# Moving statistics and GpSimd sums behind TensorE's inputs in a four-layer graph kernel, memsets to VectorE, and the last batch taken tile by tile

## The chip, the cores and the metric

The kernel runs on one core of a Trainium2 chip. The metric is the device time of one execution in microseconds. A core has TensorE (PE in the profile; its weight loads are PEld), VectorE (DVE), ScalarE (ACT), GpSimd (POOL) and SyncE (SP), which here issues all the transfers. Each engine works through its own queue in order and waits at an instruction until that instruction's inputs are there.

## What is computed

The input x has 32 batches of 512 tokens with 128 features; adj is a 512 by 512 matrix. Four layers follow each other, each of the form x = x + f(relu(layernorm(x))), with layernorm over the features:

```python
# layer 0: A = softmax of an edge table spread over adj; M = identity
out = einsum('ij,bjg->big', A * M, h @ W[0]) + einsum('ij,bjg->big', A * (1 - M), h @ W[1]) + bias
# layer 1: two Chebyshev hops with adj (both matrices are adj, so terms are shared)
out = relu(concat(h, adj_T h, (2 adj_T adj_T - 1) h, ...) @ Theta1 + bias)
# layer 2: weights = adj * adj, elementwise
features = relu(h @ psi_w + psi_b); messages = einsum('nm,bnd->bmd', weights, features)
out = relu(concat(messages, h) @ phi1_w + phi1_b) @ phi2_w + phi2_b
# layer 3: attention
A = exp(8 * tanh((h @ q) (h @ k)^T / sqrt(128) / 8)) * adj; out = (A / rowsum(A)) @ h @ v
```

## The kernel before

Two batches make a pair; there are 16 pairs (NQ = 16), q or r counting them. Tokens lie in four tiles (NT = 4) of 128 partitions. All matrix products are f32.

A layer's work on a pair is: statistics of each token (`stats_steps`: four BATCH_NORM_STATS2 on VectorE, L197, a square root on ScalarE, L209, a reciprocal and one multiply on VectorE, L211 and L212); the normalised tile h (eight activations on ScalarE, L225); a turn to feature-major hT (`turn_steps`: two VectorE transposes, L259, and a trip through DRAM); then matrix products. The statistics for the next layer are taken when a layer has updated x.

The products with the 512 by 512 matrices use Strassen's scheme with seven products in place of eight. `right_steps` (L300, GpSimd) makes four sums of blocks of the moving side; `sum_steps` (L285) makes four sums of blocks of the matrix, once for each matrix. `products` runs the seven in a fixed order, 1, 6, 5, 7, 2, 4, 3, over three PSUM banks a, c, d. Products 6, 7 and 4 share bank c, so product 7 (the fourth in order) can only start when VectorE has read product 6 out of the bank, and that reading adds what was read of product 1.

The run has two parts.

Up to L917 the order on each engine is the source's order. It prepares the attention matrix and runs layer 0 pair by pair in `round0(r)`, r = 0 to 14. In a round, `evict` reads the products: for product 1, L693 on VectorE adds the bias into u and L694 on GpSimd adds it to x; for product 6, L696 and L697; for product 7, L701, L702 and L703; products 2, 4 and 3 get a second part from `diagonal` (L684 on TensorE, with the tiles hd) and are added to x in L706, L709 and L712; a last diagonal is added in L764. hd of the next pair is made by `diagonal_of` (L636, GpSimd, two multiplications of 128 by 512). Between the products, the source puts in slices of other pairs' work with `go(steps, n)`: `ahead[q]` are the statistics for layer 0 of pair q from 4 on, `stats5` is `ahead[r + 5]`, `own[r]` the statistics of the pair just finished, `nxt` the block sums for round r + 1. From round 4 on, `sums_ahead` makes one sum of the adj or cheb matrix on GpSimd per round; layer 1 uses these.

After L917 a planner orders the instructions, with the order of the source as priority. `layer1`, `layer2` and `layer3` are generators, one for each pair; a loop at the end starts one more pair in each step and lets each active generator go on to its next `yield`. Layer 1 of pair 15 and layer 2 of pair 0 start in the same step. In `layer1` the last stage is the projection, y (L814), the update of x (L815), and `ln_stats`. In `layer2` the names are feat (projection p_feat on TensorE, L828 on VectorE, relu L829 on ScalarE), rt_feat (the block sums on GpSimd), msgT (the seven products, evicted by ScalarE L337 and L345 and VectorE L339, L341, L347, L349, L356), and h1T (L845 on ScalarE, from p_phi, L843 and L844). In `layer3` each batch has qkh and hv in one tile (copies L863 and L868 on VectorE, a column of ones for the row sums set by a memset, L867), the scores (p_score L873, tanh L874, exp L876), the product with adj (L878, by turns on VectorE and GpSimd), and p_av (L886), divided by its row sum (L888 reciprocal, L891 multiply and add) and stored.

Of the kernel before, what the change touches and what calls it, by code (L numbers as in the profile page):

```python
# [24 lines left out]
def kernel(  # L25
# [37 lines left out]
    nc = tc.nc  # L63
    B, N, D = x.shape
    NT = N // P
    NE = e_l0.shape[1]
    NK = NE // P
    NQ = B // 2
# [8 lines left out]
    def bank(name):  # L77
        return psum.tile([P, 512], F32, tag="bank", name=name)
# [27 lines left out]
    xt = []  # L106
# [80 lines left out]
    def ln_stats(q):  # L187
        for _ in stats_steps(q):
            pass
# [190 lines left out]
    def bias(q):  # L380
        x11 = xt[q][:, 0, 0:2, :]
        nc.gpsimd.tensor_add(x11, x11, spread(b0, 2))
# [14 lines left out]
    def go(steps, n=99):  # L397
        for _ in range(n):
            if next(steps, steps) is steps:
                return  # L400
# [125 lines left out]
    p = bank("p_qk_t")  # L526
# [51 lines left out]
    p = bank("p_qk")  # L578
# [28 lines left out]
    p = bank("p_adiag")  # L607
# [43 lines left out]
    ahead = {q: stats_steps(q) for q in range(4, NQ)}  # L651
# [17 lines left out]
    def diagonal_of(q):  # L669
        src = hT[f"hT0_{q}"] if q > 2 else hT[q]  # L670
        hd[q] = [straight(src, b, adiag, f"hd_{q}_{b}") for b in range(2)]

    def round0(r):

        now = rights.pop(r)

        def x_of(I, b):
            return xt[r][:, b, 2 * I : 2 * I + 2, :]  # L680

        def diagonal(p, I, b, first):
            for i in range(2):
                nc.tensor.matmul(p[:, i * D : (i + 1) * D], hd[r][b][:, blk(2 * I + i)], w0[:, 0, :],  # L684
                                 start=(first and i == 0), stop=True, skip_group_check=True)

        u = work.tile([P, 3, 2, D], F32, tag="u", name=f"u_l0_{r}", bufs=2)
        held = {}

        def evict(k, p):  # L690
            pv = p[:, :H].rearrange("p (i f) -> p i f", i=2)
            if k == 1:
                nc.vector.tensor_add(u[:, 0], pv, spread(b0, 2))  # L693
                nc.gpsimd.tensor_add(x_of(1, 0), x_of(1, 0), u[:, 0])  # L694
            elif k == 6:
                nc.vector.tensor_add(u[:, 1], pv, u[:, 0])  # L696
                nc.gpsimd.tensor_add(x_of(0, 1), x_of(0, 1), u[:, 1])  # L697
            elif k == 5:
                held["d"] = pv
            elif k == 7:  # L700
                nc.vector.tensor_add(u[:, 2], pv, u[:, 0])  # L701
                nc.vector.tensor_add(u[:, 2], held["d"], u[:, 2])  # L702
                nc.gpsimd.tensor_add(x_of(1, 1), x_of(1, 1), u[:, 2])  # L703
            elif k == 2:
                diagonal(p, 0, 0, False)
                nc.vector.tensor_add(x_of(0, 0), pv, x_of(0, 0))  # L706
            elif k == 4:
                diagonal(p, 1, 0, False)
                nc.vector.tensor_add(x_of(1, 0), pv, x_of(1, 0))  # L709
            elif k == 3:  # L710
                diagonal(p, 0, 1, False)
                nc.vector.tensor_add(x_of(0, 1), pv, x_of(0, 1))  # L712

        stats5 = ahead.get(r + 5, iter(()))
        nxt = right_of(r + 1) if r + 1 < NQ else iter(())
        if r == 0:
            diagonal_of(0)
            go(ln[3])
            go(pieces[2])
            h[3] = normed_tile(3)  # L720
            normal3 = normed_steps(3, h[3])
            go(normal3, 4)
            go(ahead[4], 2)
        else:
            if r + 4 < NQ:
                normalise(r + 4)
            go(own[r - 1], 1)
            go(nxt, 2)
        for i, _ in enumerate(products(f"l0_{r}", by_token, sums["att"], now, evict)):
            if i == 0:  # L730
                if r == 0:
                    go(ahead[4], 2)
                else:
                    go(stats5, 1)
            elif i == 1:
                if r == 0:
                    go(stats5, 2)
                else:
                    go(nxt)
                    if r + 3 < NQ:  # L740
                        turn(r + 3)
            elif i == 2:
                go(stats5, 1)
            elif i == 3 and r == 0:
                go(stats5, 1)
            elif i == 4:
                if r == 0:
                    go(turned[2], 1)
                    go(turned[2])
                    go(normal3)  # L750
                    go(ahead[4], 1)
                    go(stats5, 1)
                else:
                    if r + 3 < NQ:
                        go(turn(r + 3))
                    go(own.pop(r - 1))
            elif i == 5:
                if r == 0:
                    turn(3)
                else:  # L760
                    go(stats5, 2)
        p = bank(f"p_l0_{r}_e")
        diagonal(p, 1, 1, True)
        nc.vector.tensor_add(x_of(1, 1), p[:, :H].rearrange("p (i f) -> p i f", i=2), x_of(1, 1))  # L764
        own[r] = stats_steps(r)
        if r == 0:
            go(turn(3))
            go(nxt)
            go(own[r], NT)
            go(ahead[4])  # L770
        go(stats5)
        if r > 0:
            go(own[r], NT)
        if r + 2 < NQ:
            go(projection(r + 2))
        if r == 0:
            normalise(4)
        if r < 2:
            go(pieces[3], 1)
        elif r == 2:  # L780
            go(pieces[3])
        if r + 1 < NQ:
            bias(r + 1)
            if r >= 4:
                go(sums_ahead, 1)
            diagonal_of(r + 1)
        if r == 3:
            nc.gpsimd.tensor_add(th12, th[:, 1:3, :], th[:, 3:5, :])
        if r + NQ // 2 < NQ:
            loads(r + NQ // 2)  # L790
# [6 lines left out]
    def layer1(q):  # L797
        h = normed(q)
        yield
        hT = transposed(h, f"hT1_{q}")  # L800
        right = right_blocks(lambda J, b: h[:, b, 2 * J : 2 * J + 2, :], f"h_{q}", [nc.gpsimd] * 4)
        yield
        x1T = pair_tile(f"x1T_{q}").rearrange("p (b w) -> p b w", b=2)
        x2T = pair_tile(f"x2T_{q}").rearrange("p (b w) -> p b w", b=2)
        mixes = (mixed(f"x1T_{q}", sums["adj"], right, x1T), mixed(f"x2T_{q}", sums["cheb"], right, x2T))
        for _ in zip(*mixes):
            pass
        hs = [straight(hT, b, None, f"hs_{q}_{b}") for b in range(2)]
        yield
        for b in range(2):  # L810
            po = projected(f"p_l1_{q}_{b}", (columns(hs[b]), th[:, 0, :]), (columns(x1T[:, b]), th12[:, 0, :]),
                           (columns(x2T[:, b]), th12[:, 1, :]))
            y = late.tile([P, NT, D], F32, tag="y", name=f"y1_{q}_{b}", bufs=2)
            nc.vector.tensor_add(y, po, spread(b1, NT))  # L814
            nc.vector.scalar_tensor_tensor(xt[q][:, b], y, 0.0, xt[q][:, b], OP.max, OP.add)  # L815
        ln_stats(q)

    def layer2(q):
# [33 lines left out]
    def layer3(q):  # L852
# [5 lines left out]
        for b in range(2):  # L858
# [5 lines left out]

            pv = projected(f"p_hv_{q}_{b}", (at(hT, b), vw))
            hv = both[:, N : N + NT * (D + 1)].rearrange("p (t f) -> p t f", f=D + 1)
            nc.gpsimd.memset(hv[:, :, D : D + 1], 1.0)  # L867
            nc.vector.tensor_copy(hv[:, :, :D], pv)  # L868
            yield
            ex = square_tile(f"ex_{q}_{b}")  # L870
# [8 lines left out]
            yield  # L879
            out_r = out[2 * q + b].rearrange("(t p) f -> p t f", p=P)  # L880
            rsum = stats.tile([P, NT], F32, tag="rsum", name=f"rsum_{q}_{b}", bufs=4)
            for i0 in range(0, NT, 2):
                po = bank(f"p_av_{q}_{b}_{i0}").rearrange("p (i f) -> p i f", i=2)
                for i in range(2):
                    for t in range(NT):
                        nc.tensor.matmul(po[:, i, : D + 1], ex[:, t, blk(i0 + i)], hv[:, t, :],  # L886
                                         start=(t == 0), stop=(t == NT - 1))
                nc.vector.reciprocal(rsum[:, i0 : i0 + 2], po[:, :, D])  # L888
                for i in range(2):
                    xi = xt[q][:, b, i0 + i, :]  # L890
                    nc.vector.scalar_tensor_tensor(xi, po[:, i, :D], rsum[:, i0 + i : i0 + i + 1], xi,  # L891
                                                   OP.mult, OP.add)
                if b == 1 and q == NQ - 1:
                    nc.sync.dma_start(out_r[:, i0 : i0 + 2, :], xt[q][:, b, i0 : i0 + 2, :])
            if not (b == 1 and q == NQ - 1):
                nc.sync.dma_start(out_r, xt[q][:, b])

    adjTx = []
# [67 lines left out]
```

## Time and profile before

| What | Value |
|---|---|
| time, median of 3 runs | 980.47 us (980.4 to 980.68) |
| span of the profiled run | 979.2 us |
| time of the profiled run | 981.21 us |
| granted TensorE clock | 1.0 |
| f32 rate of TensorE, read from the starts | 0.89 us for 8 matmuls of 128 columns, 0.86 us for 4 of 256 |
| layer 0 rounds | from 40 to 196 us |
| layers 1, 2 and 3 | from 196, 475 and 686 us |

How it is read: the page gives each engine's busy time, a matmul's end being modelled. A list of waits names, for each instruction, the time that its engine stood idle just before it and which instruction's semaphore ended that. A timeline prints start, duration, engine, line, operation, output and inputs, shapes, a count of merged instructions, and in brackets the idle time before with its releaser. Where an instruction waits for several semaphores, the last one is named, and the name can be wrong if that engine only happened to finish then.

### The profile page before, as it was taken

What the parts mean: (1) busy time and instruction counts of PE and PEld (TensorE: products, weight loads), DVE (VectorE), ACT (ScalarE), POOL (GpSimd) and SP (SyncE); (2) the same over time, 40 slices, a digit from 0 to 9 for tenths busy, and PEclk for the clock granted to TensorE, in tenths of its full rate; (3) what the DMA queues carried; (4) which work ended last, traced back from release to release, by engine and by line L of the source; (5) the groups of instructions that cost most, each with busy time, mean ns of one, the idle gap of its engine ahead of it and who ended that gap; (6) DMA issues with size and microseconds to landing.
All of it is one profiled execution on the core that took longest, in us unless ns stands there. A gap on an engine that the chain in (4) does not pass through costs nothing.

```text
span 979.2 us, 16183 instructions
## 1 busy us (share of the span) xinstructions
PE 966.5 (99%) x5925; PEld 802.1 (82%) x5926; DVE 596.7 (61%) x1386; ACT 467.2 (48%) x1057; POOL 412.4 (42%) x551
## 2 busy tenths in 40 slices
PE   8999999999999999999999999999999999999998
PEld 4799999999999999999967777777667777777776
DVE  8788888755565655557566766556655444444444
ACT  3765445222322323238676544545674455444553
POOL 4778999841316313121244433344142332223322
PEclk9999999999999999999999999999999999999999
DMA  9255553522121221334343333332222121121111
GB/s 257 92 139 158 159 135 104 151 85 67 44 76 55 65 65 44 87 87 123 93 118 119 95 103 105 87 84 68 71 71 75 44 76 55 55 76 44 55 33 44
DMA packets 83023, 87.17 MB, mean 89 GB/s; under 512 B 6784, under 2 KB 73088, under 8 KB 82944
## 3 DMA queue, kind: packets, MB, share of 16 engines
q1 hardware_dynamic: 82944, 86.14, 31.4%
q8 instruction: 47, 0.77, 0.3%
q14 instruction: 32, 0.26, 0.1%
HBM read 44.70 MB, written 41.42 MB: 88 GB/s over the span
## 4 chain that ended last, share of the span: by engine, by line
PE 93%; POOL 2%; DMA 1%; ACT 1%; issue 1%; DVE 1%; SPq 0%; DVEq 0%; POOLq 0%; ACTq 0%
PE p_av L886 12%; PE p_l L372 11%; PE p_score L873 11%; PE p_msgT_c L319 4%; PE p_x2T_c L319 4%; PE p_x1T_c L319 4%; PE p_l_c L326 4%; PE p_feat L372 3%; PE p_x1T_a L319 3%; PE p_hv L372 3%; PE p_x1T_d L319 3%; PE p_x2T_d L319 3%; PE p_x2T_a L319 3%; PE p_msgT_d L319 3%; PE p_msgT_a L319 3%; PE p_qkh L860 3%
## 5 line engine op out<-in xcount | busy, mean ns | idle before, releaser
L225 ACT ACTIVATE h<-x,sh,rs 128x128 f32<-128x128 f32 x448 | 182.5, 483 | 73.2 <-PE p_x2T_d L319 43.9
L878 POOL TENSOR_TENSOR ex<-ex,adjTx 128x512 f32<-128x512 f32 x64 | 83.3, 1303 | 197.1 <-issue 147.4
L874 ACT ACTIVATE ex<-p_score 128x512 f32<-128x512 f32 x128 | 71.6, 588 | 122.9 <-issue 113.0
L886 PEld LDWEIGHTS p_av<-qkh_hv,ex 128*128 128x128 f32 x1024 | 118.4, 191 | 9.6 <-issue 7.2
L886 PE MATMUL p_av<-qkh_hv,ex 128*128 128x129 f32 x1024 | 120.3, 275 | 0.9 <-POOL qkh_hv L867 0.6
L873 PE MATMUL p_score<-qkh_hv,hT 128*128 128x512 f32 x256 | 115.2, 593 | 0.0
L259 DVE STREAM_TRANSPOSE hb_hT<-h 128x512 f32<-128x512 f32 x122 | 84.4, 698 | 19.8 <-ACT h L225 19.6
L878 DVE TENSOR_TENSOR ex<-ex,adjTx 128x512 f32<-128x512 f32 x64 | 45.9, 717 | 76.5 <-ACT ex L876 76.5
L873 PEld LDWEIGHTS p_score<-qkh_hv,hT 128*128 128x128 f32 x256 | 46.2, 190 | 46.5 <-issue 45.0
L197 DVE BATCH_NORM_STATS2 bn<-x 128x6 f32<-128x256 f32 x224 | 83.2, 417 | 1.3
L300 POOL TENSOR_TENSOR rt_h<-h 128x256 f32<-128x256 f32 x32 | 22.6, 727 | 133.4 <-PE p_x2T_c L319 133.1
L876 ACT ACTIVATE ex<-ex 128x512 f32<-128x512 f32 x128 | 76.5, 631 | 1.8
L300 POOL TENSOR_TENSOR rt_feat<-feat,feat 128x256 f32<-128x256 f32 x16 | 11.6, 727 | 128.4 <-ACT feat L829 128.4
L372 PE MATMUL p_l<-th,x2T 128*128 128x128 f32 x256 | 49.5, 275 | 0.0
L372 PE MATMUL p_l<-th,x1T 128*128 128x128 f32 x256 | 49.5, 275 | 0.0
L372 PE MATMUL p_l<-th,hs 128*128 128x128 f32 x256 | 49.5, 275 | 0.0
L372 PEld LDWEIGHTS p_hv<-vw,hT 128*128 128x128 f32 x256 | 33.6, 192 | 15.3 <-issue 8.1
L209 ACT ACTIVATE sd<-bn,eps 128x8 f32<-128x8 f32 x60 | 17.9, 300 | 56.0 <-DVE bn L197 55.0
L634 POOL COPY hs<-hT 128x512 f32<-128x512 f32 x32 | 19.6, 611 | 54.7 <-PE p_l L372 40.5
L345 ACT COPY x1T<-p_x1T_a 128x256 f32<-128x256 f32 x16 | 6.0, 372 | 74.2 <-PE p_x1T_a L319 74.2
L636 POOL TENSOR_TENSOR hd<-hT,adiag 128x512 f32<-128x512 f32 x32 | 40.6, 1287 | 1.0 <-PE p_l_e L684 1.0
L372 PEld LDWEIGHTS p_l<-th,hs 128*128 128x128 f32 x256 | 40.0, 192 | 0.8
(241 smaller groups left out, 2188.7 us busy)
## 6 DMA issues: line engine op xcount, KB each, us to landing
d_hT<-hb_hT SPq DMA_DIRECT2D x244, 128.0 KB, 2.4
hT<-d_hT SPq DMA_DIRECT2D x61, 512.0 KB, 3.7
x<-in_x_dram SPq DMA_DIRECT2D x28, 256.0 KB, 4.3
out_dram<-x SPq DMA_DIRECT2D x28, 256.0 KB, 2.3
adj_s<-in_adj_dram SPq DMA_DIRECT2D x4, 256.0 KB, 4.9
adjT_d<-adjT SPq DMA_DIRECT2D x1, 1024.0 KB
sq<-in_adj_dram SPq DMA_DIRECT2D x4, 256.0 KB
x_last<-in_x_dram SPq DMA_DIRECT2D x4, 256.0 KB
```

What stands on the lines that cost most here:

```text
L197: nc.vector.bn_stats(st[:, k].rearrange("p e s -> p (e s)"), xt[q][:, b, t : t + 2, :].rearrange("p t f -> p f t"))
L225: nc.scalar.activation(h[:, b, t, :], xt[q][:, b, t, :], AF.Relu, bias=shift[q][:, i : i + 1], scale=scale[q][:, i : i + 1])
L259: nc.vector.transpose(hb[:, :, b].rearrange("p j t r -> p t j r"), h[:, b].rearrange("p t (j c) -> p t j c", c=QR))
L319: nc.tensor.matmul(p[:, :H], b[:, k, :], a[:, k, :], start=(first and k == 0), stop=(k == 1), skip_group_check=True)
L326: nc.tensor.matmul(p[:, i * D : (i + 1) * D], a[:, k, blk(i)], b[:, k, :], start=(first and i == 0 and k == 0), stop=(k == 1), skip_group_ ...
L372: nc.tensor.matmul(p[:, blk(t)], hT(t), w, start=(i == 0), stop=(i == len(terms) - 1))
L636: nc.gpsimd.tensor_mul(split(s), src, split(scale))
L873: nc.tensor.matmul(ps, hT[:, t, b, :], qkh, start=True, stop=True)
L874: nc.scalar.activation(ex[:, t, :], ps, AF.Tanh, scale=1.0 / (8.0 * math.sqrt(D)))
L876: nc.scalar.activation(ex[:, t, :], ex[:, t, :], AF.Exp, scale=8.0)
L878: eng.tensor_mul(ex[:, t, :], ex[:, t, :], adjTx[0][:, t, :])
L886: nc.tensor.matmul(po[:, i, : D + 1], ex[:, t, blk(i0 + i)], hv[:, t, :], start=(t == 0), stop=(t == NT - 1))
```

## The change

The statistics that stood ahead of round 0's first evictions on VectorE move behind the evictions of the second and the fourth product. From round 4 on, the sum for layer 1 moves behind the hd multiplications on GpSimd. Layer 1 of pair 15 takes its statistics two steps of the loop later, so that they are not ahead of what layer 2's second pair needs. The memset of the ones column goes from GpSimd to VectorE. The last batch is divided, added and stored one tile of 128 tokens at a time and not two. The purpose is to have what TensorE waits for done first, and a shorter end.

```diff
             go(normal3, 4)
-            go(ahead[4], 2)
         else:
...
-            if i == 0:
-                if r == 0:
-                    go(ahead[4], 2)
-                else:
-                    go(stats5, 1)
+            if i == 0 and r > 0:
+                go(stats5, 1)
             elif i == 1:
                 if r == 0:
-                    go(stats5, 2)
+                    go(ahead[4], NT)
                 else:
...
-            elif i == 2:
+            elif i == 2 and r > 0:
                 go(stats5, 1)
             elif i == 3 and r == 0:
-                go(stats5, 1)
+                go(stats5, NT)
...
             bias(r + 1)
+            diagonal_of(r + 1)
             if r >= 4:
                 go(sums_ahead, 1)
-            diagonal_of(r + 1)
...
+        if q == NQ - 1:
+            yield
+            yield
         ln_stats(q)
...
-            nc.gpsimd.memset(hv[:, :, D : D + 1], 1.0)
+            nc.vector.memset(hv[:, :, D : D + 1], 1.0)
...
-            for i0 in range(0, NT, 2):
-                po = bank(f"p_av_{q}_{b}_{i0}").rearrange("p (i f) -> p i f", i=2)
-                for i in range(2):
+            final = b == 1 and q == NQ - 1
+            n = 1 if final else 2
+            for i0 in range(0, NT, n):
+                po = bank(f"p_av_{q}_{b}_{i0}").rearrange("p (i f) -> p i f", i=2)[:, :n]
+                for i in range(n):
...
-                if b == 1 and q == NQ - 1:
-                    nc.sync.dma_start(out_r[:, i0 : i0 + 2, :], xt[q][:, b, i0 : i0 + 2, :])
-            if not (b == 1 and q == NQ - 1):
+                if final:
+                    nc.sync.dma_start(out_r[:, i0, :], xt[q][:, b, i0, :])
+            if not final:
                 nc.sync.dma_start(out_r, xt[q][:, b])
```

More of the change, by code (lines that the diff above doesn't have):

```diff
@@ L887, in layer3 @@
                                          start=(t == 0), stop=(t == NT - 1))
-                nc.vector.reciprocal(rsum[:, i0 : i0 + 2], po[:, :, D])
-                for i in range(2):
+                nc.vector.reciprocal(rsum[:, i0 : i0 + n], po[:, :, D])
+                for i in range(n):
                     xi = xt[q][:, b, i0 + i, :]
```

## The prediction

> **What bounds the kernel now.** I read the page's busy shares, then TensorE's own waits, then the timelines of all engines around each wait, and the end of the run.
>
> ```profile
> PE 966.5 (99%) x5925; PEld 802.1 (82%) x5926; DVE 596.7 (61%) x1386; ACT 467.2 (48%) x1057; POOL 412.4 (42%) x551
> ```
>
> TensorE has 966.5 of 979.2 us. Only its waits can be won, and few are left:
>
> ```profile
> PE p_adjT L405 <- DMA adj_s<-in_adj_dram: 4.6, 2, 3.4
> PE p_msgT_c L319 <- POOL rt_feat L300: 1.4, 1, 1.4
> PE p_l_c L326 <- DVE u_l L696: 1.2, 1, 1.2
> PE p_av L886 <- POOL qkh_hv L867: 0.6, 1, 0.6
> PE p_l_c L326 <- POOL hd L636: 0.5, 1, 0.5
> ```
>
> The first is the load at the start, untouched here. The others are what the change aims at: layer 2, round 0, layer 3, round 4. An engine's idle time is counted from the end of the last matmul; the loss of cadence is a little larger.
>
> Round 0, timeline of VectorE, then of TensorE:
>
> ```profile
> 41.70 0.75 DVE L197 BATCH_NORM_STATS2 bn<-x 128x6 f32<-128x256 f32 x2
> 42.37 0.40 DVE L693 TENSOR_TENSOR u_l<-p_l_a,b 128x256 f32<-128x256 f32 x1
> 42.69 0.75 DVE L197 BATCH_NORM_STATS2 bn<-x 128x6 f32<-128x256 f32 x2
> 43.37 0.40 DVE L696 TENSOR_TENSOR u_l<-p_l_c,u_l 128x256 f32<-128x256 f32 x1
> ```
>
> ```profile
> 43.91 1.13 PE L326 MATMUL p_l_c<-rt_g,attT 128*128 128x128 f32 x8 [1.24 <-DVE u_l L696]
> ```
>
> Four statistics stand before the two evictions that the fourth product needs. But the next round shows the same matmul with nothing to spare, behind a VectorE queue that does not depend on TensorE:
>
> ```profile
> 52.93 0.18 DVE L211 RECIPROCAL rs<-sd 128x8 f32<-128x8 f32 x1
> 53.15 0.92 DVE L212 SCALAR_TENSOR_TENSOR sh<-bn,rs 128x8 f32<-128x8 f32 x1
> 54.21 1.08 DVE L212 SCALAR_TENSOR_TENSOR sh<-bn,rs 128x8 f32<-128x8 f32 x1
> 55.89 0.41 DVE L696 TENSOR_TENSOR u_l<-p_l_c,u_l 128x256 f32<-128x256 f32 x1
> ```
>
> ```profile
> 52.78 2.49 POOL L636 TENSOR_TENSOR hd<-hT,adiag 128x512 f32<-128x512 f32 x2
> ```
>
> L696 ends at 56.30 and its matmul starts at 56.44, where TensorE's preceding product ended (55.51 + 0.89 = 56.40).
>
> Layer 2, second pair, on VectorE, ScalarE, GpSimd and TensorE:
>
> ```profile
> 488.85 0.42 DVE L197 BATCH_NORM_STATS2 bn<-x_last 128x6 f32<-128x256 f32 x1
> 489.78 1.08 DVE L197 BATCH_NORM_STATS2 bn<-x_last 128x6 f32<-128x256 f32 x3
> 491.11 0.67 DVE L828 TENSOR_TENSOR feat<-p_feat,psib 128x512 f32<-128x512 f32 x1
> ```
>
> ```profile
> 491.74 0.69 ACT L845 ACTIVATE h1T<-p_phi,phi1b 128x512 f32<-128x512 f32 x1 [0.54 <-PE p_phi L844]
> 492.32 1.14 ACT L829 ACTIVATE feat<-feat 128x512 f32<-128x512 f32 x2
> ```
>
> ```profile
> 493.54 0.73 POOL L300 TENSOR_TENSOR rt_feat<-feat,feat 128x256 f32<-128x256 f32 x1 [8.87 <-ACT feat L829]
> ```
>
> ```profile
> 495.69 1.13 PE L319 MATMUL p_msgT_c<-sums_sq,rt_feat 128*128 128x256 f32 x4 [1.41 <-POOL rt_feat L300]
> ```
>
> The projection p_feat ran from 488.03 to 489.8, yet its first VectorE add starts at 491.11, behind the statistics of pair 15. That lateness runs through ScalarE and GpSimd to TensorE.
>
> **What the Trainium skill says.** "Perfetto Trace Analysis", Identifying the Most-Contended Engine, holds that matmul busy share doesn't measure headroom; weight loads at 82% agree, so I work from gaps in the cadence, not from the 99%. "SBUF — State Buffer", Who interferes with whom: a VectorE instruction with two SBUF inputs contends with a GpSimd instruction that reads SBUF, and the later one blocks for the whole instruction. The trace agrees: L212, 128x8 elements, takes 150 ns at best, but here 0.92 and 1.08 us, ending at 54.07 and 55.29, where the two hd multiplications of GpSimd end (half of 2.49 us each, to 54.03 and 55.27).
>
> **The change part by part.**
>
> *Round 0.* The statistics ahead[4] and stats5 go behind the evictions of the second and fourth product. VectorE is then free at 41.77 when the last sum L285 (1.22 us from 40.55) ends: L693 from 41.70 to 42.10, L696 to 42.43, and 0.14 us later, as now (43.77 to 43.91), the matmul: 42.57. That removes 43.91 - 42.57 = 1.34 us. The eight statistics then fill VectorE to about 46, before L706, for which nobody waits; TensorE keeps the lead (0.1 us less at p_g, since ScalarE's copies of hT sit behind normalisations that wait for GpSimd's sh at 46.78) and reaches round 1's fourth product near 55.2. There L696 still ends at 56.30. Its queue: the second transpose L259 at 50.99 waits for ScalarE's h, which waited for sh, which GpSimd makes after hd(0); GpSimd has no idle time over 0.1 us from 34 to 57; then 1.38 us of own statistics, and L212 twice blocked by hd(1). None of it is moved. I cost this edit at 0: the wait returns one round later, 1.2 us long.
>
> *Rounds 4 and later.* hd goes before the sum L285. hd for round 5 ends at 98.22; its first reader, L684, starts at 100.11, so hd has no one waiting. The sums are read in layer 1 only. VectorE's L212 is blocked at a round's end by whichever GpSimd operation is running, and the two are alike (a sum 1.27 to 1.30, an hd 1.26 to 1.27), so the boundaries stay. Total of the small waits in rounds 5 to 15: under 1 us. The wait of round 4 itself (TensorE at 88.33) lies before the first sum (94.46), and L696, which ended at 88.18, explains it better than the named hd. Taken: 0, from -0.7 to +0.3.
>
> *Layer 2.* The statistics of pair 15 go two steps later, four at some 0.34 us apart. Four products wait: TensorE wanted p_msgT_c at 493.25 + 0.86 = 494.11 and got it at 495.69 (1.58); restarted at 0.96 in place of 0.86 (0.10); its next p_msgT_c, wanted at 497.51, came at 497.75 (0.24) and again restarted slowly (0.10). Sum 2.02. After: L815 of the second batch at 488.97 (now 489.19), L349 at 489.6, the two adds L828 at 489.9 and 490.5, done 491.15. ScalarE then has feat ready at 490.6 and 491.2, before h1T at 491.74, and should take both first: done 491.8. GpSimd starts at 491.9; its third operation, the one that TensorE needs (2.09 us after the start, 493.54 to 495.63), ends at 494.0, just before 494.11. I take 1.9 of 2.02. The moved statistics have a home: VectorE is idle from 494.92 to 497.27, and pair 15's next reader comes many steps later.
>
> *Memsets to VectorE.* 32 of 104 ns leave GpSimd. In layer 3 the wait at 702.27 is laid to one, but it ran at 702.15, just behind the multiplication that ended at 702.22 and that TensorE needs; the memset for this tile ran at 681.8. On VectorE no row shows it: between 65 ns, an estimate from the page "VectorE: DVE Perf Modes", The TRN2 errata (58 cycles plus the elements, at 0.96 GHz), and 172 ns, the longest reciprocal of 128x2 (L888). I take 0.1; 3.2 us in all, hidden in VectorE's idle time of layer 3 (busy 4 to 5 tenths, 76.5 us of waits before L878 alone). The buffer's wait is on long finished matmuls. On the path: 0.
>
> *Last batch by tiles.* Now the last reciprocal starts at 975.52 and two multiply-adds end at 976.34; with one tile it is one, ending at 976.08 (0.26 less). The last transfer is 64 KB for 128 KB: its packets now occupy the DMA engines from 977.2 to 977.85, half of which is 0.3. The rest of the 2.8 us from issue at 976.40 to the end of the span stays; "DMA: Bandwidth & Descriptors", Latency and other measured facts, calls a cost near 2 us fixed, which fits. Sum: 0.55, from 0.26 to 0.7. Four banks for two, of eight in turn: all long read.
>
> Sum: 980.47 - 0 - 0 - 1.9 - 0 - 0.55 = 978.0.
>
> **The rivals.**
> Half of layer 2: the order there is planned, not written out; if h1T keeps its place before the second feat, that feat ends at 492.9, GpSimd's third at 495.1, and only 0.55 is won: 980.47 - 0.55 - 0.55 = 979.4. For it: ScalarE takes h1T first now. Against: feat was then not ready; it would be.
> Round 0 pays: if L212 slipped in before hd, or round 1 had slack that I miss, 1.3 more: 976.7. Against: L211 waits for ScalarE at 52.6 and hd starts at 52.78.
> Slower: a new plan. From 575 to 682 TensorE loses about 0.24 per pair in msgT, behind ScalarE's order; the first pairs don't. Six more such pairs cost 1.4; moved statistics that meet the next eviction some 0.5; memsets queued ahead of L863 up to 3.2. With little won in layer 2: near 982.
>
> **How the numbers follow.** The forecast 0.55, half of layer 2 0.2, round 0 pays 0.12, slower 0.13. 0.2% is 1.96 us, so 978.51. Of the forecast's share 0.05 falls short of that, of the slower one 0.02 ends within: faster 0.50 + 0.12 = 0.62, same 0.05 + 0.20 + 0.02 = 0.27, slower 0.11. The range, 976.5 to 980.2, holds the first three; it leaves out the slower and a little beside.
>
> **What would show it.** No wait near 43.9, but one of about 1.2 us before the fourth product of round 1, ended by L696. p_msgT_c of the second pair within 0.2 us of its cadence, feat before h1T on ScalarE. The waits at 88 and 702 unchanged. Last transfer 64 KB, the time from the last matmul to the end shorter by about 0.55. I am wrong if round 1 does not wait, if the wait of layer 2 stays over 0.5 us, or if msgT or layer 3 show new waits.

## The result, and the profile after

| | before | after |
|---|---|---|
| time, median | 980.65 us (980.4 to 981.49, 6 runs) | 977.92 us (977.47 to 978.87, 6 runs) |
| ratio | | 0.9971, 95% interval 0.9958 to 0.9984 |
| span of the profiled run | 979.2 us | 976.0 us |

The forecast was 978.0 us. Of the 3.2 us between the two profiled spans, some 1.5 are no effect of the change: the part ahead of round 0 took 39.83 us in the one and 38.29 in the other. The difference arises in the first 22 us, where no edit acts; most of it is the load of adj that TensorE waits for (in the list below 3.3 us of waiting, where it was 4.6), and another run of the changed kernel took 39.23. So I compare stages, and not the two spans.

The page's busy shares of the changed kernel, then its list of TensorE's waits (engine and line waiting, what ended it, us in total, times, longest):

```profile
PE 965.5 (99%) x5925; PEld 802.1 (82%) x5926; DVE 596.1 (61%) x1420; ACT 467.5 (48%) x1057; POOL 411.3 (42%) x519
```

```profile
PE p_adjT L405 <- DMA adj_s<-in_adj_dram: 3.3, 1, 3.3
PE p_l_c L326 <- DVE u_l L696: 2.6, 2, 1.6
PE p_av L887 <- POOL ex L877: 0.8, 2, 0.6
PE p_msgT_c L319 <- DVE u_msgT L339: 0.3, 1, 0.3
```

The engine totals say next to nothing: 1 us less on TensorE, 32 memsets moved. The waits say more. The 1.4 us of rt_feat in layer 2 are gone. The wait for L696 has not gone: it was 1.2 us once, in round 0, and is now 2.6 us in two places, rounds 1 and 4. (Round 4's wait, 0.5 us, stood in the list before under the name of hd.)

To add up such losses I use the loss of cadence: for every matmul, how much later it started after the one before than that kind normally does, summed by stage where it is over 0.04 us. It includes the slow restart: behind a wait TensorE loses another 0.07 to 0.10 us within the product itself. "End" is from the last matmul's end to the end of the span.

| us | layer 0: round 0 | round 1 | round 4 | layer 0 in all | layer 2 | layer 3 | end |
|---|---|---|---|---|---|---|---|
| before | 1.48 | 0.07 | 0.69 | 3.20 | 4.08 | 1.91 | 3.71 |
| after | 0.38 | 1.24 | 1.88 | 3.95 | 2.43 | 1.91 | 2.99 |

Round 1 first. TensorE before, the fourth product of round 1 without a wait; then TensorE in the changed kernel at the same place, and VectorE and GpSimd ahead of it:

```profile
56.44 1.13 PE L326 MATMUL p_l_c<-rt_g,attT 128*128 128x128 f32 x8
```

```profile
52.88 1.06 PE L326 MATMUL p_l_d<-rt_g,sums_att 128*128 128x128 f32 x8
54.95 1.13 PE L326 MATMUL p_l_c<-rt_g,attT 128*128 128x128 f32 x8 [1.01 <-DVE u_l L696]
```

```profile
51.66 0.92 DVE L212 SCALAR_TENSOR_TENSOR sh<-bn,rs 128x8 f32<-128x8 f32 x1
52.72 1.08 DVE L212 SCALAR_TENSOR_TENSOR sh<-bn,rs 128x8 f32<-128x8 f32 x1
54.40 0.40 DVE L696 TENSOR_TENSOR u_l<-p_l_c,u_l 128x256 f32<-128x256 f32 x1
```

```profile
51.27 2.51 POOL L636 TENSOR_TENSOR hd<-hT,adiag 128x512 f32<-128x512 f32 x2
```

The same two L212, 0.92 and 1.08 us long against the two halves of hd, and L696 behind them. Round 0 gave 1.10 us and round 1 took 1.17.

Layer 2, second pair, on VectorE, ScalarE, GpSimd and TensorE:

```profile
488.93 1.28 DVE L827 TENSOR_TENSOR feat<-p_feat,psib 128x512 f32<-128x512 f32 x2
490.13 1.43 DVE L197 BATCH_NORM_STATS2 bn<-x_last 128x6 f32<-128x256 f32 x4
```

```profile
489.73 1.21 ACT L828 ACTIVATE feat<-feat 128x512 f32<-128x512 f32 x2 [3.70 <-DVE feat L827]
490.90 0.69 ACT L844 ACTIVATE h1T<-p_phi,phi1b 128x512 f32<-128x512 f32 x1
```

```profile
491.02 0.73 POOL L300 TENSOR_TENSOR rt_feat<-feat,feat 128x256 f32<-128x256 f32 x1 [7.17 <-ACT feat L828]
```

```profile
492.41 1.03 PE L319 MATMUL p_msgT_a<-sq,feat 128*128 128x256 f32 x4
493.27 1.03 PE L319 MATMUL p_msgT_c<-sums_sq,rt_feat 128*128 128x256 f32 x4
```

The adds come before the statistics, ScalarE takes both feat before h1T, and p_msgT_c starts 0.86 us after p_msgT_a: exactly its cadence.

The end, VectorE's last two lines, before and after:

```profile
975.52 0.17 DVE L888 RECIPROCAL rsum<-p_av 128x2 f32<-128x2 f32 x1 [0.97 <-PE p_av L886]
975.73 0.61 DVE L891 SCALAR_TENSOR_TENSOR x_last<-p_av,rsum,x_last 128x128 f32<-128x128 f32 x2
```

```profile
973.04 0.17 DVE L889 RECIPROCAL rsum<-p_av 128x1 f32<-128x1 f32 x1 [0.34 <-PE p_av L887]
973.24 0.35 DVE L892 SCALAR_TENSOR_TENSOR x_last<-p_av,rsum,x_last 128x128 f32<-128x128 f32 x1
```

One multiply-add follows the last reciprocal, where there were two.

### The profile page after: what moved, and what is told of

Its sections match the earlier page's. It is cut to its first block, busy times and chain, and to the rows that moved or that the text cites. A ratio compares the mean times of both kernels' runs of the same rounds, so it can differ in the third digit from the quotient of the medians.

```text
span 976.0 us, 16214 instructions
## 1 busy us (share of the span) xinstructions
PE 965.5 (99%) x5925; PEld 802.1 (82%) x5926; DVE 596.1 (61%) x1420; ACT 467.5 (48%) x1057; POOL 411.3 (42%) x519
## 4 chain that ended last, share of the span: by engine, by line
PE 90%; DVE 3%; POOL 3%; ACT 1%; issue 1%; DMA 1%; DVEq 0%; POOLq 0%; ACTq 0%
PE p_av L887 12%; PE p_l L372 11%; PE p_score L872 11%; PE p_msgT_c L319 4%; PE p_x2T_c L319 4%; PE p_x1T_c L319 4%; PE p_l_c L326 4%; PE p_feat L372 3%; PE p_x1T_a L319 3%; PE p_hv L372 3%; PE p_x1T_d L319 3%; PE p_x2T_d L319 3%; PE p_x2T_a L319 3%; PE p_msgT_d L319 3%; PE p_msgT_a L319 3%; PE p_qkh L859 3%
## 5 line engine op out<-in xcount | busy, mean ns | idle before, releaser
L225 ACT ACTIVATE h<-x,sh,rs 128x128 f32<-128x128 f32 x448 | 182.5, 483 | 74.0 <-PE p_x2T_d L319 43.9
```

The lines of the kernel that those rows point to most:

```text
L225: nc.scalar.activation(h[:, b, t, :], xt[q][:, b, t, :], AF.Relu, bias=shift[q][:, i : i + 1], scale=scale[q][:, i : i + 1])
```

## The experiments

The theory: layer 2 and the end carry the gain, round 0's edit only moves a wait by one round, the memset and the order of sums and hd are off the path. The rivals: each of the other parts pays or costs something of its own, which the sum hides. The first five kernels are the kernel before with one part of the change each.

**Round 0 alone.**

```diff
-            go(ahead[4], 2)
...
-                if r == 0:
-                    go(ahead[4], 2)
-                else:
-                    go(stats5, 1)
+            if i == 0 and r > 0:
+                go(stats5, 1)
...
-                    go(stats5, 2)
+                    go(ahead[4], NT)
...
             elif i == 3 and r == 0:
-                go(stats5, 1)
+                go(stats5, NT)
```

> The kernel before with round 0's edit alone. Theory (the wait returns): TensorE's wait before the fourth product of round 0 falls from 1.4 us to about 0.3, and round 1's fourth product, which had none, waits about 1.2 us behind L696; time within 0.3 us of before. Rival (round 0 pays): round 1 has no wait and the time falls by 1.1 to 1.3 us.

Measured: 980.98 us (13 runs) beside 981.51 (48 runs), ratio 0.9996, interval 0.9988 to 1.0004. Loss in layer 0 3.23 us, before 3.20: round 0 down from 1.48 to 0.35, round 1 up from 0.07 to 1.23. TensorE, fourth product of round 1:

```profile
55.16 1.02 PE L326 MATMUL p_l_c<-rt_g,attT 128*128 128x128 f32 x7 [0.99 <-DVE u_l L696]
```

On time the edit by itself brings nothing that can be told from the scatter, and in the trace its saving turns up as a loss in the next round.

**The statistics of pair 15 alone** (the two yields).

```diff
+        if q == NQ - 1:
+            yield
+            yield
         ln_stats(q)
```

> The kernel before with the two yields of layer 1 alone. Theory: the four waits of the second pair in layer 2 (2.0 us together) are gone, both feat activations stand before h1T on ScalarE, and the time falls by 1.6 to 2.0 us. Rival (half of layer 2): h1T stays ahead of the second feat, 0.6 us or less. Rival (it is the end or the start that gave the gain): no change.

Measured: 979.49 us (12 runs) beside 981.51, ratio 0.9981, interval 0.9973 to 0.9989. Layer 2 loses 2.38 us in place of 4.08, and its length falls from 211.2 to 209.5. The four losses of the second pair, 2.02 us, are gone; a msgT wait near 574, 0.21 us with its slow restart before, grew to 0.56. Net 1.7 us, without any other part of the change. Why the later wait grew was not tried.

**The order of sum and hd alone.**

```diff
             bias(r + 1)
+            diagonal_of(r + 1)
             if r >= 4:
                 go(sums_ahead, 1)
-            diagonal_of(r + 1)
```

> The kernel before with hd ahead of the sums from round 4 on alone. Theory: nobody waits for hd; the wait of round 4 itself, which lies before the first sum, stays what chance makes it (0.7 or 1.9 us), the small waits of rounds 5 to 15 change by less than 0.7 us, the time by less than 0.5. Rival (the swap shifts the cost to round 4): round 4 waits 1.9 us here, and the time grows by about 1 us.

Measured: 981.34 us (13 runs) beside 981.51, ratio 1.0, interval 0.9992 to 1.0008. In its profiled run round 4 waited 1.78 us, as in the changed kernel, and the kernel with only the end changed, which has the old order, waited 1.79. So the order is not what makes that wait long. From 90 to 190 us, behind round 4, its trace loses 0.15 us, and the kernel before 0.68. More of this comes with the last experiment below.

**The last batch by tiles alone** (the same lines as in the change).

```diff
-            for i0 in range(0, NT, 2):
+            final = b == 1 and q == NQ - 1
+            n = 1 if final else 2
+            for i0 in range(0, NT, n):
...
-                    nc.sync.dma_start(out_r[:, i0 : i0 + 2, :], xt[q][:, b, i0 : i0 + 2, :])
+                    nc.sync.dma_start(out_r[:, i0, :], xt[q][:, b, i0, :])
```

> The kernel before with the last batch by tiles alone. Theory: from the last matmul's end to the span's end 3.0 us in place of 3.7, nothing else moves, and the time falls by 0.6 to 0.7 us. Rival (four transfers in place of two queue on SyncE): the end is no shorter than 3.5 us.

Measured: 980.06 us (21 runs) beside 981.51, ratio 0.9989, interval 0.9982 to 0.9995. From the last matmul's end to the end of the span 3.00 us, before 3.71: 0.71 won. The length of layer 3 falls by the same 0.7, from 293.12 to 292.40.

**The memset alone.**

```diff
-            nc.gpsimd.memset(hv[:, :, D : D + 1], 1.0)
+            nc.vector.memset(hv[:, :, D : D + 1], 1.0)
```

> The kernel before with the memset on VectorE alone. Theory: the wait of 0.6 us before the first p_av stays, now laid to the multiplication L878 of GpSimd, and the time is within 0.3 us of before. Rival (the memset was the cause): that wait is gone and 0.6 us with it.

Measured: 983.79 us (980.85 to 987.31, 14 runs) beside 981.51 (980.01 to 986.81, 20 runs), ratio 1.0005, interval 0.9987 to 1.0022. On time this is inconclusive. Its trace loses 8.25 us in layer 0, which ends long before the first memset of layer 3, and 1.91 in layer 3, as ever. Of the 5.05 us more in layer 0, 1.2 are a longer wait in round 4 and 3.9 are two waits of 2 us, ending at 101 and 133. This is what VectorE and GpSimd did ahead of the first of these two:

```profile
95.70 3.16 DVE L212 SCALAR_TENSOR_TENSOR sh<-bn,rs 128x8 f32<-128x8 f32 x1
```

```profile
95.66 2.50 POOL L636 TENSOR_TENSOR hd<-hT,adiag 128x512 f32<-128x512 f32 x2
98.11 0.73 POOL L300 TENSOR_TENSOR rt_g<-g 128x256 f32<-128x256 f32 x1
```

A multiply of 128 by 8 elements took 3.16 us. It started 40 ns behind hd and ended, at 98.86, with the third GpSimd instruction (98.84; the line of hd holds two). Each of the traces so far has the same pair of instructions, L212 and hd, ahead of round 4, and there the two nearly tie. In the profile before L212 starts first:

```profile
85.68 0.17 DVE L212 SCALAR_TENSOR_TENSOR sh<-bn,rs 128x8 f32<-128x8 f32 x1
```

```profile
85.72 2.50 POOL L636 TENSOR_TENSOR hd<-hT,adiag 128x512 f32<-128x512 f32 x2
```

```profile
88.33 1.13 PE L326 MATMUL p_l_c<-rt_g,attT 128*128 128x128 f32 x8 [0.45 <-POOL hd L636]
```

and in the profile after it also starts first, 36 ns ahead where it was 39, and still is held until the first half of hd is done:

```profile
84.22 1.33 DVE L212 SCALAR_TENSOR_TENSOR sh<-bn,rs 128x8 f32<-128x8 f32 x1
```

```profile
84.25 2.50 POOL L636 TENSOR_TENSOR hd<-hT,adiag 128x512 f32<-128x512 f32 x2
```

```profile
88.02 1.13 PE L326 MATMUL p_l_c<-rt_g,attT 128*128 128x128 f32 x8 [1.64 <-DVE u_l L696]
```

In both VectorE then runs without a pause up to the end of L696, 2.50 us after L212's start before and 3.66 after, so that the time for which L212 is held reaches TensorE. Of the seven traces so far four have the long form, 1.78 to 1.80 us of loss at this matmul, its slow restart not counted (after, order alone, end alone, memset alone), and three the short, 0.61 (before, round 0 alone, pair 15 alone). Nothing in the edits sorts them: two of the long ones, the end alone and the memset alone, differ from the kernel before in layer 3 only. What sorts them is L212 ahead of round 4, held for 1.33 to 1.34 us in the four and done in 0.17 in the three. The next kernels take the collisions away.

**The statistics of pair 5 later**, on the changed kernel: L211 and L212 of pair 5 go from the end of round 0, and the normalisation on ScalarE that follows them from the start of round 1, to behind the second product of round 1.

```diff
-            if r + 4 < NQ:
+            if r > 1 and r + 4 < NQ:
                 normalise(r + 4)
...
+                    if r == 1:
+                        go(ahead[5])
+                        normalise(5)
...
-        go(stats5)
         if r > 0:
+            go(stats5)
             go(own[r], NT)
```

> The changed kernel, with the last step of pair 5's statistics (L211, L212) and its normalisation moved from the end of round 0 to behind product 6 of round 1. Theory (round 1 waits because L212 is blocked by hd ahead of L693 and L696): round 1's wait falls from 1.2 us to 0.3 or less, and the time by about 1 us against the changed kernel (near 977), if round 4 is the same. Rival (round 1 waits for something else, ScalarE or GpSimd): its wait stays over 0.8 us.

Measured: 977.17 us (7 runs) beside 981.51, ratio 0.9939, interval 0.9918 to 0.9961 (the medians alone give 0.9956; the kernel before scattered up to 986.81 beside it, and that pulls the ratio down). Round 4 took its short form, 0.62. Round 1 has no wait; VectorE and TensorE there:

```profile
54.49 0.39 DVE L696 TENSOR_TENSOR u_l<-p_l_c,u_l 128x256 f32<-128x256 f32 x1
54.81 0.18 DVE L211 RECIPROCAL rs<-sd 128x8 f32<-128x8 f32 x1
55.03 0.78 DVE L212 SCALAR_TENSOR_TENSOR sh<-bn,rs 128x8 f32<-128x8 f32 x1
```

```profile
54.21 1.06 PE L326 MATMUL p_l_d<-rt_g,sums_att 128*128 128x128 f32 x8
55.11 1.06 PE L326 MATMUL p_l_c<-rt_g,attT 128*128 128x128 f32 x8
```

With one L212 out of L696's way the fourth product follows the third after 0.9 us, without a gap. The normalisation moved too, but in the changed kernel VectorE ran without a pause from 49.50 to the end of L696, so it was VectorE's own queue, and not ScalarE, that made L696 late. This is the part that round 0's edit lacked.

**The Chebyshev matrix earlier**, on the changed kernel: the last piece of it goes from the end of round 2 to its start, because GpSimd stood still before it in the changed kernel, for a ScalarE copy (L418) queued behind those of g, and then ran without a pause into round 4:

```profile
75.07 0.46 POOL L419 TENSOR_TENSOR cheb<-cheb,ident 128x128 f32<-128x128 f32 x1 [5.73 <-ACT cheb L418]
75.49 0.73 POOL L382 TENSOR_TENSOR x<-x,b 128x256 f32<-128x256 f32 x1
```

```diff
+            if r == 2:
+                go(pieces[3])
             go(own[r - 1], 1)
...
-        elif r == 2:
-            go(pieces[3])
```

> The changed kernel, with the last cheb row block's eviction (ScalarE L418, GpSimd L419) moved from the end of round 2 to its start, so that GpSimd does not stand 5.7 us before it. Theory (round 4 waits because GpSimd's additions of round 3 and with them L764, L212 and L696 come late): round 4's wait of 1.8 us (0.6 in the run before) is under 0.2, and the time is 0.7 to 1.9 us less than the changed kernel's, near 976.5. Rival (round 4's wait is of the statistics or hd themselves): it stays over 0.5 us.

Measured: 976.76 us (6 runs), ratio 0.9937, interval 0.9912 to 0.9961. L419 ran at 68.22 in place of 75.07. Round 4 has no wait, round 1 keeps its 1.22 us; layer 0 loses 2.18. The changed kernel was not run beside these two kernels; that follows below.

**Both.**

> The changed kernel with both moves of the two kernels before it. Theory: rounds 1 and 4 both without a wait over 0.3 us; time 2 to 3 us under the changed kernel's, near 975.5. Rival (a wait moves on again): a new wait of about 1 us in rounds 2 to 6, time as with one of the moves alone.

Measured: 975.7 us (6 runs), ratio 0.9926, interval 0.9902 to 0.995. Layer 0 loses 0.96 us. The kernel before varied by 7 us beside these, so four more kernels were run beside each other on one chip, the first two as they stand above:

> The changed kernel, beside the three variants below on one chip, so that they can be compared with it and not only with the kernel before. My theory: 2.7 us under the kernel before, and 2 us over the kernel with both further moves, because of two waits in layer 0, 1.2 us in round 1 always and 0.6 or 1.8 in round 4 by chance. Rival: the waits only look expensive and TensorE catches up elsewhere; then all four kernels are within 0.5 us.

> The changed kernel with both further moves, once more, now beside the changed kernel. My theory: 1.8 to 2.4 us less than the changed kernel in the same call, with no wait over 0.6 us in rounds 1 to 14, and the narrower spread of times. Rival: the difference seen before came from another chip or call, and is under 0.5 us.

| kernel | median | runs |
|---|---|---|
| before | 981.2 | 11, 980.12 to 983.12 |
| changed | 977.47 | 5, 977.29 to 979.4 |
| changed, both further moves | 975.58 | 5, 975.32 to 976.68 |

The ratios to the kernel before are 0.9965 (0.9952 to 0.9978) and 0.9944 (0.9932 to 0.9955). The two further moves bring 1.9 us more; the five times of each do not overlap. Losses in layer 0: 3.87 and 0.71 us. With both, this version beats both kernels of the case.

**The memset back on GpSimd**, on the kernel with both moves, where layer 0 no longer drowns it:

```diff
-            nc.vector.memset(hv[:, :, D : D + 1], 1.0)
+            nc.gpsimd.memset(hv[:, :, D : D + 1], 1.0)
```

> Both further moves, with the memset of the ones column back on GpSimd. With layer 0 free of its waits, what is left of the spread should be small enough to see this edit. My theory (off the path on either engine): within 0.3 us of the kernel with both moves, and the first wait before p_av the same 0.35 us. Rival (the memset stood in TensorE's way): 0.5 us or more slower, with that wait longer.

Measured: 975.51 us (974.97 to 977.01, 5 runs) against 975.58: no difference. TensorE at the first p_av with the memset on GpSimd:

```profile
695.83 1.04 PE L890 MATMUL p_av<-qkh_hv,ex 128*128 128x129 f32 x4 [0.18 <-POOL ex L880]
697.51 1.72 PE L890 MATMUL p_av<-qkh_hv,ex 128*128 128x129 f32 x13 [0.64 <-POOL qkh_hv L869]
```

The same 0.64 us is laid to the memset here and to the multiplication (ex) in the changed kernel. The name in the bracket was an accident of which of the two ended last; the wait was for the multiplication in both.

**The order of sum and hd put back**, on the kernel with both moves (the third experiment's edit reversed).

> Both further moves, with the sum for layer 1 ahead of the hd multiplications again, in rounds 4 and later. My theory: 0 to 0.5 us slower, with small waits of some 0.2 us back in the rounds from 5 to 11. Rival (the order decides round 4's wait and more): over 1 us slower. Other rival: no difference.

Measured: 976.65 us (975.62 to 979.04, 6 runs) against 975.58 (975.32 to 976.68). Slower by 1.1 us in the medians; the ranges overlap, but the upper half of these times, 976.97 to 979.04, lies above all five of the other kernel. Six times against five do not settle a difference of this size. The profiled run is the 979.04 one, the slowest. GpSimd, VectorE and TensorE at its round 8:

```profile
119.96 1.32 POOL L285 TENSOR_TENSOR sums_adj<-adj_s,sums_adj 128x512 f32<-128x512 f32 x1
121.21 2.52 POOL L636 TENSOR_TENSOR hd<-hT,adiag 128x512 f32<-128x512 f32 x2
```

```profile
120.09 3.66 DVE L212 SCALAR_TENSOR_TENSOR sh<-bn,rs 128x8 f32<-128x8 f32 x1
```

```profile
128.19 1.02 PE L326 MATMUL p_l_c<-rt_g,attT 128*128 128x128 f32 x7 [1.77 <-DVE u_l L696]
```

and GpSimd and VectorE at the same place with hd first:

```profile
119.20 1.27 POOL L636 TENSOR_TENSOR hd<-hT,adiag 128x512 f32<-128x512 f32 x1
120.95 1.27 POOL L636 TENSOR_TENSOR hd<-hT,adiag 128x512 f32<-128x512 f32 x1 [0.48 <-PE p_l_e L684]
122.18 1.29 POOL L285 TENSOR_TENSOR sums_adj<-adj_s,sums_adj 128x512 f32<-128x512 f32 x1
```

```profile
119.01 0.26 DVE L212 SCALAR_TENSOR_TENSOR sh<-bn,rs 128x8 f32<-128x8 f32 x1
121.55 0.70 DVE L212 SCALAR_TENSOR_TENSOR sh<-bn,rs 128x8 f32<-128x8 f32 x1
```

Put first, hd comes early enough that its second half must wait 0.48 us for TensorE's last diagonal (L684) to be through with the buffer. The rounds are then alike: from 92 to 160 us every L212 takes either 0.25 to 0.28 or 0.70 us, and no matmul waits. With the sum first GpSimd runs the three without a pause, and L212 takes anything from 0.17 to 3.66 us in the same stretch.

The other traces say the same of the order. Loss of cadence from 90 to 190 us, behind round 4:

| order in rounds 4 and later | traces | loss, us |
|---|---|---|
| sum first | 6: before, round 0, pair 15, end and memset alone, and this one | 0.68 to 0.72 in four; 2.8 (this one) and 4.5 (memset alone) |
| hd first | 8: all others | 0 to 0.27 |

So hd first saves some 0.5 us in the common case, and waits of 2 us in this stretch were met only with the sum first.

## Why the prediction was right

**The sum.** The forecast was a gain of 2.45 us. By the stages of the traces it is 1.7 in layer 2 and 0.72 at the end, 2.4; the medians say 2.73, and the interval of the ratio allows 1.6 to 4.1. Layer 0 was taken as unchanged; its two traces differ by 0.75 the other way: rounds 0 and 1 lose 0.07 more and round 4 1.19 more, by the tie described above, and the rounds behind lose 0.5 less, by the order. That the median came within 0.1 us of 978.0 is therefore in part luck: the error of layer 2 and that of the end nearly cancel, and the gain of the order and round 4's two forms are in the times without being in the sum.

**Round 0, costed at 0: right, for the reason given.** The wait of 1.24 us went, and one of 1.01 us, ended by L696, stood before the fourth product of round 1. The edit alone gave 0.9996, and taking one L212 away from ahead of L696 removed the wait. Not quite right was "no wait near 43.9": in every trace with this edit 0.28 to 0.56 us of loss stayed at that matmul.

**Layer 2, 1.9 of 2.02: mechanism right, the size a little high.** The order on ScalarE, feat, feat, h1T, was as forecast, and p_msgT_c kept its cadence, so that all 2.02 us of the second pair were won. The term left out of the sum was the later wait of msgT near 574, which took 0.35 to 0.37 back.

**Memsets, 0 on the path: right.** They take 62 ns on VectorE, min and max alike, close to the 65 ns that I had estimated from the Trainium skill, "VectorE: DVE Perf Modes", The TRN2 errata, and far from the upper bound of 172. The view of the line:

```profile
L866 DVE MEMSET qkh_hv<- x32: 62/62/62, 682.5 to 946.2; 128x4 f32 x32
```

With the engine exchanged in the steadier kernel the times are 975.58 and 975.51, and the wait of 0.64 us stays.

**The last batch, 0.55: undersized, 0.72 measured.** The 0.26 us of VectorE are there (one multiply-add in place of two). The other term, half of the time that the last packets occupied the DMA engines, 0.3, is then worth 0.46. By the traces the last packet ended 1.47 us after the issue before and 1.19 after the change, which is the forecast's 0.3; from there to the end of the span it was 1.33 and is 1.19. Why this last piece shrank, no run tells.

**Rounds 4 and later, 0: the wrong step, though its cost hid.** I argued that a sum and an hd last equally long, "so the boundaries stay", and that the wait at 88 was "unchanged". The first left out that hd must wait for TensorE's last diagonal to free its buffer: put first it makes a pause in GpSimd's queue, of 0.37 to 0.52 us in ten rounds of the kernel with both moves, and with the sum first such a pause is left only in the last two of them, so the boundaries move. That it is the pause that lets L212 in is my reading; no run makes the pause without the order. In the traces the order is worth some 0.5 us, and more where a wait of 2 us is met; in the medians 1.1 us where layer 0 has no other waits, which six runs against five do not settle, and nothing on the kernel before by itself (ratio 1.0, 0.9992 to 1.0008). The second missed that the wait at 88 is not one number: 0.61 or 1.8 us, by whether L212 or hd, which start within 50 ns of each other, is held; no part of the change touches this pair. The forecast took one value of it for a constant; the times before and after both contain that toss.

## What to carry to other kernels

A wait that an edit removes is won only if the next instruction of the same kind was not waiting just behind it: look one round further at the same matmul, and at whether the queue that ends its wait depends on TensorE at all. In this kernel a short VectorE instruction with two SBUF inputs, ahead of an eviction, cost up to 2 us of TensorE's time where GpSimd ran a row of long instructions; moving it behind the eviction (round 1), or moving some of GpSimd's work to an earlier place (round 4), removed the wait. When a kernel's times scatter by several us, take away what scatters first, and compare small edits on the steadier kernel.

## What the runs showed of the hardware

The Trainium skill, "SBUF — State Buffer", Who interferes with whom, says that VectorE with two SBUF inputs contends with a GpSimd instruction that reads SBUF, and of the shared ports that the one that issues first has them for its whole instruction while the other fully blocks. The runs agree that it blocks, and show that it can last longer than one instruction: L212, 0.15 to 0.17 us at its shortest, took 1.33 us against one GpSimd instruction and 3.16 and 3.66 us against three in a row, ending 20 ns after the third in both cases. In round 1 of the changed kernel, by contrast, the first L212 (51.66 to 52.58) was let in between the two halves of hd, the first of which ended at 52.55. And the recorded start does not decide. Ahead of round 4, in the nine traces that have this pair, L212 starts 33 to 47 ns before hd: five times it was held (33 to 47 ns), four times it took 0.17 us (37 to 47 ns). What lets VectorE in at one boundary and not at another was not tried, and stays open.
